# Taking GpSimd out of a four-layer graph network: its sums on VectorE, its powers as Ln and Exp on ScalarE with a Newton step

## The chip, the cores and the metric

The kernel runs on one core of a Trainium2 chip. The metric is the device time of one execution in microseconds, the median of several runs. The profile is one further execution, recorded instruction by instruction.

## The reference

32 independent graphs of 512 nodes with 256 features go through four layers. Each layer starts from `h = relu(layernorm(x))` and adds its result to `x`.

```python
# layers 0, 1, 2: attention over the neighbours (adj > 0), each with its own score
#   0: four heads, leaky_relu(e_src[i] + e_dst[j]), softmax over j, elu
#   1: one head, the same, but softmax over i, elu
#   2: scores h diag(a_k) h^T, leaky_relu, softmax over j
# layer 3: a transformer block over the symmetric adjacency
qkv = h @ Wqkv.T + bqkv                       # 8 heads of 32
attn = softmax(where(allowed, (q * scale) @ k.T, -inf))
x1 = layernorm(h + (attn @ v) @ Wo.T + bo) * g1 + b1
x2 = layernorm(x1 + relu(x1 @ W1.T + b1f) @ W2.T + b2f) * g2 + b2
```

A layernorm needs `(var + eps) ** -0.5` for each row. There are six per graph: one ahead of each of the four layers and the two inside layer 3.

## The kernel before, in words

One graph is 512 x 256 numbers, held as a tile of 128 partitions x 4 row blocks x 256. Everything of a graph stays on the chip. The body is written as a plan: `quick_path` (L307) calls `plan.dve`, `plan.act`, `plan.pool`, `plan.dma` and `plan.matmuls` (L213 to L240) for each step of each graph. Nothing is issued then. Each step takes the next number of the table `PLACES` (L265), and `carry_out` (L173) sorts the steps of all graphs by that number plus 100000 for each graph and issues them in that order. So the order on each engine is fixed by a table that was made beforehand from assumed durations (the arguments `fixed`, `each`, `takes`, `moves`); at run time each engine takes its own queue strictly in order and waits on semaphores. The numbers of one graph reach to five rounds of 100000, so that some five graphs are in flight at any time, in different layers. All instructions of the plan carry the line of the shared helper: L208 for VectorE, ScalarE and GpSimd, L240 for transposes and L242 for products on TensorE, L229 for the DMAs of the SP queue.

The places that the change touches:

- `norm_stats` (L418), called by `normed` (L433) for all six layernorms. VectorE takes statistics of the four row blocks (`st`, `mv`). GpSimd adds eps and raises to -0.5 (`rstd`, two instructions on 128 x 4). VectorE forms `shift` = -mean * rstd. ScalarE then applies `func(rstd * t + shift)` to each row block (`h`, `n` or `y`), and for five of the six norms TensorE transposes the result (`ps_t`).
- `layer2` (L599): GpSimd sets one column of `h` to 1.
- `layer3` (L646): GpSimd adds the bias rows to `h` and to `x`, multiplies `n` by the first gain and adds the first bias, multiplies `y` by the second gain and adds `x`. These are six instructions per graph on 128 x 1024 numbers.
- the heads of `layer3`, two groups (`g` = 0, 1) of four. For each of four blocks `j`: four score products into two PSUM tiles `ps_s`, two exponentials on ScalarE to `p`, one masking product on VectorE, then four products into `ps_ct` (the sums of values) and four with ones into `ps_to` (the softmax sums, each repeated on 32 partitions). ScalarE then copies `ps_to` to `to` and `ps_ct` to `cT`. The four distinct rows of `to` go through DRAM into a tile of 128 x 16 (`part`), VectorE inverts that, it goes through DRAM again and comes back repeated on 32 partitions by four DMAs (`inv<-in_d`), and VectorE multiplies `cT` by it. `ps_wo` is the product that follows.

PSUM holds two tiles for layers 0 to 2 (`ps_a`), two for layer 3 (`ps_b`), one `ps_ct` and one `ps_to`. Both `ps_b` tiles are taken by the scores of one block `j`.

A second path, `general_path`, runs only if a range check (`ok`) fails at the end. It does not run with these inputs.

Of the kernel before, what the change touches and what calls it, by code (L numbers as in the profile page):

```python
# [11 lines left out]
F32 = mybir.dt.float32  # L12
# [3 lines left out]
AF = mybir.ActivationFunctionType  # L16
OP = mybir.AluOpType
AX = mybir.AxisListType

P = 128  # L20
EPS = 1e-5
# [101 lines left out]
class Plan:  # L123
# [99 lines left out]
    def dma(self, out, in_, moves, takes=0.1, how="dma_start"):  # L223

        pairs = list(zip(out, in_)) if isinstance(out, list) else [(out, in_)]
        outs = [o for o, _ in pairs if isinstance(o, Part)]
        ins = [i for _, i in pairs if isinstance(i, Part)]
        real = lambda x: x.real() if isinstance(x, Part) else x
        call = lambda: [getattr(self.nc.sync, how)(real(o), real(i)) for o, i in pairs]  # L229
        return self.put("SP", takes * len(pairs), 0.1, outs, ins, call, moves=moves)  # L230
# [19 lines left out]
def cut(i, n):  # L250
    return slice(i * n, (i + 1) * n)
# [6 lines left out]
def width(args):  # L258
# [7 lines left out]
    5095, 0, 75421, 87257, 75421, 75422, 79730, 91873, 132389, 236254, 196081, 207636, 243857, 181976, 44107,  # L266
    34440, 42508, 30766, 53912, 52376, 46625, 51110, 60213, 60213, 60213, 70466, 70613, 70954, 70954, 70466,
    70613, 70954, 70955, 75749, 70466, 71304, 71304, 77395, 77395, 82751, 82751, 82751, 85231, 85616, 86620,
    87570, 88383, 87584, 87624, 87664, 87664, 90673, 88473, 88474, 90343, 90415, 90674, 90415, 94498, 90674,
    90674, 90675, 93427, 103844, 106136, 116456, 117561, 120303, 122479, 122479, 123102, 124701, 126554,  # L270
    118952, 128436, 123749, 129193, 132446, 132770, 134171, 134171, 134497, 134497, 125538, 135514, 135152,
    129427, 140054, 141849, 142365, 143295, 150203, 150647, 145729, 145510, 143627, 145727, 146676, 152577,
    152577, 154799, 155729, 155729, 160482, 161143, 161214, 199191, 252294, 161472, 170438, 163168, 161214,
    172243, 180822, 179815, 182438, 187335, 190423, 220320, 232349, 231107, 233547, 233849, 232349, 232349,
    233799, 233849, 233849, 234567, 235455, 235455, 235455, 237246, 238660, 238660, 238660, 237541, 238502,
    238502, 239837, 240015, 240584, 237049, 237247, 237247, 240584, 241849, 243910, 241849, 245067, 249595,
    249623, 249943, 256299, 263793, 272483, 276199, 251185, 257754, 261671, 261953, 275753, 249971, 249971,
    249971, 254481, 274656, 250485, 259697, 260833, 261106, 261106, 280063, 280063, 280502, 280588, 280588,
    280957, 280957, 281766, 282382, 283125, 280221, 279419, 284381, 281071, 281440, 284267, 283125, 283472,
    281561, 284267, 284087, 288386, 288386, 288386, 289738, 293577, 293577, 293145, 292388, 294294, 294650,  # L280
    294650, 295508, 295951, 296386, 296387, 296820, 297407, 295508, 298258, 298315, 298315, 299004, 299120,
    301865, 305936, 306664, 308000, 310488, 311544, 299530, 302461, 303130, 307485, 307981, 315988, 316802,
    318221, 312505, 310558, 310559, 316547, 317146, 318296, 321032, 321616, 318341, 308129, 308850, 313424,
    313654, 314031, 328211, 328128, 328971, 328971, 324764, 324951, 324951, 329855, 331034, 331034, 330095,
    332212, 332212, 350464, 363968, 329929, 325975, 334039, 341986, 331621, 325975, 336262, 347783, 347783,
    347783, 349528, 351433, 349793, 349596, 349528, 356201, 356201, 356202, 356822, 357899, 357954, 357954,
    360273, 360273, 362490, 363814, 363814, 363814, 363814, 363814, 363814, 364260, 364260, 375184, 377819,
    380031, 379751, 364470, 364941, 364941, 367324, 368254, 375151, 376257, 377227, 378857, 380372, 381525,
    381525, 381525, 384251, 383694, 381824, 383733, 382666, 387368, 389194, 390503, 386847, 389476, 387536,
    389476, 395301, 398014, 391945, 394211, 395296, 400302, 402208, 403099, 414392, 404840, 420693, 428278,  # L290
    428491, 430754, 431986, 433030, 399143, 399518, 399143, 406475, 409183, 415116, 404886, 411811, 410216,
    411811, 416520, 417484, 414099, 418232, 416703, 420289, 430404, 424852, 420322, 420706, 422850, 422850,
    432328, 425058, 425376, 432362, 429007, 430005, 430005, 431322, 432006, 433711, 364606, 433030, 434739,
    435922, 436329, 436329, 436344, 436344, 436344, 436345, 429961, 430544, 430005, 430005, 438443, 437988,
    440014, 440373, 440373, 440373, 441792, 441792, 441792, 442528, 442528, 442528, 442528, 442528, 442716,
    442529, 442529, 442529, 442529, 442529, 442529, 442806, 442823, 442823, 443009, 451286, 451286, 443789,
    443789, 443789, 446989, 448875, 447063, 450551, 451265, 451501, 453552, 456094, 453552, 447255, 448150,
    448695, 448695, 451068, 452896, 453703, 455669, 456461, 456752, 456909, 457770, 451242, 451242, 463337,
    463337, 463485, 463558, 463559, 463559, 463559, 463559, 463789, 463789, 463789, 463789, 463789, 463789,
    463789, 457995, 457995, 457995, 457995, 457995, 457996, 457996, 457996, 457996, 457996, 457996, 457996,  # L300
    458410, 458410, 458410, 458410, 458410, 463790, 463790, 458795, 458795, 463790, 463790, 458795, 458795,
    463790, 463790, 463790, 467483, 470996, 470996, 472513, 476280, 476333, 506480,
# [4 lines left out]
def quick_path(  # L307
# [5 lines left out]
    nc = tc.nc  # L313
    B, N, D = x.shape
    NT = N // P
# [26 lines left out]
    K |= {tag: Kind(act, tag, slots) for tag, slots in dict(st=8, mv=8, rstd=8, shift=8, spr=3).items()}  # L342
# [5 lines left out]
    def new(tag, name, shape, dtype=F32):  # L348
        return plan.tile(K[tag], name, shape, dtype)
# [6 lines left out]
    nhalf = const.tile([P, NT], F32, name="nhalf")  # L356
    nc.gpsimd.memset(nhalf, -0.5)
# [60 lines left out]
    def norm_stats(t):  # L418

        st = new("st", "st", [P, NT, 6])  # L420
        mv = new("mv", "mv", [P, NT, 2])
        for i in range(NT):
            plan.dve("bn_stats", st[:, i], t[:, i], fixed=0.4)
        for i in range(NT):
            plan.dve("bn_aggr", mv[:, i], st[:, i])
        rstd = new("rstd", "rstd", [P, NT])
        plan.pool("tensor_scalar_add", rstd, mv[:, :, 1], EPS, fixed=0.22)
        plan.pool("tensor_tensor", rstd, rstd, nhalf, OP.pow, fixed=1.03)
        shift = new("shift", "shift", [P, NT])
        plan.dve("scalar_tensor_tensor", shift, mv[:, :, 0], -1.0, rstd, OP.mult, OP.mult)  # L430
        return rstd, shift
# [51 lines left out]
    def masks(b, adj_t):  # L483
# [7 lines left out]
        for i in range(NT):  # L491
            plan.dma(mT[:, :, cut(i, P)], m[:, i], 0.5, 1.2, "dma_start_transpose")
# [106 lines left out]
    def layer2(b, x_t, mT):  # L599
        h = new("h1", f"h2_{b}", [P, NT, D + 1])  # L600
        plan.pool("memset", h[:, :, D], 1.0)
# [44 lines left out]
    def layer3(b, x_t, m3):  # L646
# [5 lines left out]
        plan.pool("tensor_add", h, h, bo_r.unsqueeze(1).to_broadcast([P, NT, D]))  # L652
# [23 lines left out]
        for g in range(KD):  # L676
            ps_ct = new("ps_ct", "ps_ct", [P, N])
            ps_to = new("ps_to", "ps_to", [P, N])
            for j in range(NT):
# [22 lines left out]
                plan.matmuls(0.98, *((ps_to[at], ones, p[:, r], j == 0, j == NT - 1) for r, at in enumerate(heads)))  # L702
            to = new("to", "to", [P, N])
            plan.act("copy", to, ps_to)
            plan.act("copy", cT[:, g], ps_ct)


# [4 lines left out]
            plan.dve("reciprocal", part, part, each=7.5e-3, fixed=0.13)  # L712
            parts.append(part)
            d2 = new("in_d", "in_d", [HG, N])
            plan.dma(d2.flat(lambda d: d.rearrange("r (q n) -> (r q) n", q=HD)), part, 0.05)
            inv = new("inv3", "inv3", [P, N])

            plan.dma(
                [inv[r * HD : (r + 1) * HD] for r in range(HG)],
                [d2[r].flat(lambda d, r=r: bass.AP(tensor=d.tensor, offset=d.offset, ap=[[0, HD], [1, N]])) for r in range(HG)],  # L720
                0.9,
            )
            plan.dve("tensor_mul", cT[:, g], cT[:, g], inv)
        plan.pool("tensor_add", x_t, x_t, b2_r.unsqueeze(1).to_broadcast([P, NT, D]))
# [16 lines left out]
        plan.pool("tensor_mul", n, n, g1_r.unsqueeze(1).to_broadcast([P, NT, D]))  # L741
        plan.pool("tensor_add", n, n, b1_r.unsqueeze(1).to_broadcast([P, NT, D]))
# [23 lines left out]
        plan.pool("tensor_mul", y, y, g2_r.unsqueeze(1).to_broadcast([P, NT, D]))  # L766
        plan.pool("tensor_add", y, y, x_t)
# [506 lines left out]
```

## Time and profile before

| what | value |
|---|---|
| median of 3 runs | 3963.26 us (3956.66 to 3964.89) |
| the profiled execution's own time | 3974.49 us |
| its span, first to last instruction | 3972.7 us |
| TensorE busy | 3757.4 us, 95% |
| VectorE busy | 2550.2 us, 64% |
| ScalarE busy | 1829.4 us, 46% |
| GpSimd busy | 772.2 us, 19% |
| mean share of the 16 DMA engines that the main queue takes | 12.8% |
| one graph to the next in the middle of the run (start of the mask step to the next) | 117.4 us |

A row of the groups gives line, engine, operation, names and shapes, count; then the busy time in us and the mean of one in ns; then the idle time of the engine just before these instructions and what ended it. "<-" in a wait reads "waited for". "issue" is idle time for which the profile shows no cause. In a timeline row the first number is the start in us, the second the time.

### The profile page before, as it was taken

The page shows a single profiled execution, that of the slowest core. Times are in us where ns is not written, and L with a number is a line of the kernel's source. Part 1 is how long each engine was busy: PE and PEld are TensorE (multiplying, and loading weights), DVE is VectorE, ACT ScalarE, POOL GpSimd, SP SyncE. Part 2 cuts the span into 40 slices and gives each one's busy share as a digit, 9 for nine tenths or more (in the row PEclk, how much of TensorE's full clock was granted, in tenths as well). Part 3 has the DMA queues.
Part 4 walks back from the last instruction along what each step waited for, and adds up shares of the span by engine and source line. Part 5 has one row for each costly group of instructions (what it writes and reads, how often), then busy time and mean ns, then how long its engine had stood idle before and what let it go on. Part 6 is the DMA issues. An engine that isn't in the chain of part 4 may idle for free. (4 is left out here: it accounts for less than half of the span.)

```text
span 3972.7 us, 51876 instructions
## 1 busy us (share of the span) xinstructions
PE 3757.4 (95%) x19974; PEld 2349.5 (59%) x19974; DVE 2550.2 (64%) x5083; ACT 1829.4 (46%) x3297; POOL 772.2 (19%) x618
## 2 busy tenths in 40 slices
PE   4899999999999999999999999999999999999986
PEld 3655666565666565566655566656566656566543
DVE  3576667766667676666776666676666776666532
ACT  1245444545444545544454544454544455454432
POOL 0012211212221121221121221121221121222121
PEclk7799999999999999999999999999999999999998
DMA  3111101111101111101111101111111111110000
GB/s 114 54 44 43 37 28 45 49 44 43 44 21 45 49 49 44 43 17 48 45 49 44 43 17 48 45 49 44 43 34 31 45 49 48 41 31 17 17 12 12
DMA packets 168911, 161.41 MB, mean 41 GB/s; under 512 B 98640, under 2 KB 134992, under 8 KB 164560
## 3 DMA queue, kind: packets, MB, share of 16 engines
q1 hardware_dynamic: 162304, 153.02, 12.8%
q10 hardware_dynamic: 6352, 4.99, 0.4%
q8 instruction: 160, 2.62, 0.3%
q14 instruction: 95, 0.78, 0.1%
HBM read 122.96 MB, written 18.22 MB: 36 GB/s over the span
## 5 line engine op out<-in xcount | busy, mean ns | idle before, releaser
L242 PEld LDWEIGHTS ps_o<-wh,p 128*128 128x128 f32 x5120 | 713.4, 199 | 157.8 <-issue 80.8
L242 PE MATMUL ps_o<-wh,p 128*128 128x65 f32 (+1 forms) x5120 | 761.1, 302 | 23.2 <-DVE p L208 21.2
L208 DVE TENSOR_TENSOR p<-p,m 128x2048 f32<-128x2048 f32 x256 | 585.6, 2288 | 74.1 <-ACT p L208 71.0
L208 ACT ACTIVATE p<-ps_s 128x1024 f32<-128x1024 f32 x512 | 506.3, 1024 | 213.6 <-PE ps_s L242 142.4
L242 PE MATMUL ps_f<-ff_t,f 128*128 128x256 f32 x2048 | 458.2, 380 | 36.2 <-DVE o L208 35.0
L208 POOL TENSOR_SCALAR rstd<-mv 128x4 f32<-128x4 f32 x192 | 47.8, 249 | 2276.8 <-DVE mv L208 2125.2
L242 PE MATMUL ps_f<-tT,ff_t 128*128 128x512 f32 x1024 | 481.2, 604 | 3.4 <-ACT tT L208 2.6
L242 PEld LDWEIGHTS ps_f<-ff_t,f 128*128 128x128 f32 x2048 | 381.9, 190 | 111.5 <-issue 61.2
L208 DVE SCALAR_TENSOR_TENSOR p<-rows,rt,mT 128x512 f32<-128x512 f32 x512 | 367.2, 744 | 42.3 <-PE ps_o L242 28.2
L208 ACT ACTIVATE h<-x,shift,rstd 128x256 f32<-128x256 f32 x512 | 274.9, 595 | 182.5 <-PE ps_o L242 144.0
L208 ACT ACTIVATE f<-ps_f,ff1b_c 128x512 f32<-128x512 f32 x256 | 164.4, 681 | 368.8 <-PE ps_f L242 368.7
L242 PE MATMUL ps_s<-qk 32*128 32x512 f32 x2048 | 295.1, 641 | 2.6 <-ACT qk L208 1.5
L242 PEld LDWEIGHTS ps_f<-tT,ff_t 128*128 128x128 f32 x1024 | 184.2, 192 | 170.5 <-issue 137.7
L242 PE MATMUL ps_to<-p,ones 128*32 128x512 f32 x2048 | 268.0, 606 | 6.0 <-DVE p L208 6.0
L242 PE MATMUL ps_ct<-p,v 128*32 128x512 f32 x2048 | 267.5, 606 | 5.2 <-DVE p L208 5.2
L208 POOL TENSOR_TENSOR rstd<-rstd,nhalf 128x4 f32<-128x4 f32 x192 | 258.0, 1348 | 13.4
L240 PE MATMUL ps_t<-ident,h 128*128 128x128 f32 x1024 | 203.8, 294 | 57.4 <-ACT h L208 38.7
L240 PEld LDWEIGHTS ps_t<-ident,h 128*128 128x128 f32 x1024 | 126.8, 146 | 208.7 <-ACT h L208 110.8
L208 DVE TENSOR_TENSOR u<-ps_f,n 128x512 f32<-128x512 f32 x64 | 43.7, 683 | 321.5 <-PE ps_t L240 284.3
L208 DVE SCALAR_TENSOR_TENSOR shift<-mv,rstd 128x4 f32<-128x4 f32 x192 | 161.0, 839 | 125.8 <-POOL rstd L208 125.8
L242 PE MATMUL ps_o<-h,p 128*128 128x257 f32 x1024 | 239.5, 386 | 0.9 <-DVE x L208 0.9
L242 PE MATMUL ps_qk<-h3T,wqkv_t 128*128 128x512 f32 x512 | 237.5, 597 | 1.1 <-ACT h3T L208 1.1
(114 smaller groups left out, 4885.8 us busy)
## 6 DMA issues: line engine op xcount, KB each, us to landing
adj<-in_adj_dram SPq DMA_DIRECT2D x32, 1024.0 KB
rows<-rows_d SPq DMA_DIRECT2D x32, 1024.0 KB
x<-in_x_dram SPq DMA_DIRECT2D x32, 512.0 KB
rows<-rows_d SPq DMA_DIRECT2D x32, 512.0 KB
inv<-in_d SPq DMA_DIRECT2D x256, 64.0 KB
out_dram<-y SPq DMA_DIRECT2D x32, 512.0 KB
ff_t<-in_L_gnn_W_dram ACTq DMA_DIRECT2D x2, 1024.0 KB
mT<-m SPq DMA_TRANSPOSE x128
```

The lines of the kernel that those rows point to most:

```text
L208: return [getattr(unit, method)(*map(real, args), **{k: real(v) for k, v in kw.items()})]
L240: made.append(self.nc.tensor.transpose(*map(real, c)))
L242: made.append(self.nc.tensor.matmul(*map(real, c[:3]), start=c[3], stop=c[4]))
```

## The change

All of it is inside `quick_path`. `PLACES` is a new table: another fixed order for all engines, made from the new assumed costs.

```diff
-    def dma(self, out, in_, moves, takes=0.1, how="dma_start"):
+    def dma(self, out, in_, moves, takes=0.45, how="dma_start"):
 PLACES = [
...
-    nhalf = const.tile([P, NT], F32, name="nhalf")
-    nc.gpsimd.memset(nhalf, -0.5)
+    eps = const.tile([P, 1], F32, name="eps")
+    nc.gpsimd.memset(eps, EPS)
...
         rstd = new("rstd", "rstd", [P, NT])
-        plan.pool("tensor_scalar_add", rstd, mv[:, :, 1], EPS, fixed=0.22)
-        plan.pool("tensor_tensor", rstd, rstd, nhalf, OP.pow, fixed=1.03)
+        plan.act("activation", rstd, mv[:, :, 1], AF.Ln, bias=eps, fixed=0.27)
+        plan.act("activation", rstd, rstd, AF.Exp, scale=-0.5)
+        r = new("newton", "newton", [P, NT])
+        plan.dve("scalar_tensor_tensor", r, mv[:, :, 1], EPS, rstd, OP.add, OP.mult)
+        plan.dve("scalar_tensor_tensor", r, r, -0.5, rstd, OP.mult, OP.mult)
+        plan.dve("scalar_tensor_tensor", rstd, r, 1.5, rstd, OP.add, OP.mult)
+
+        plan.dve("scalar_tensor_tensor", ok[:, :NT], mv[:, :, 1], 2.0**60, ok[:, :NT], OP.is_le, OP.mult)
         shift = new("shift", "shift", [P, NT])
...
-            plan.dma(mT[:, :, cut(i, P)], m[:, i], 0.5, 1.2, "dma_start_transpose")
+            plan.dma(mT[:, :, cut(i, P)], m[:, i], 0.5, 1.3, "dma_start_transpose")
...
-        plan.pool("memset", h[:, :, D], 1.0)
+        plan.dve("memset", h[:, :, D], 1.0)
...
-        plan.pool("tensor_add", h, h, bo_r.unsqueeze(1).to_broadcast([P, NT, D]))
+        plan.dve("tensor_add", h, h, bo_r.unsqueeze(1).to_broadcast([P, NT, D]))
...
+            last = g == KD - 1
+            inv = new("inv3", "inv3", [P, N])
+            if last:
+                for half in (slice(0, N // 2), slice(N // 2, N)):
+                    plan.dve("reciprocal", inv[:, half], ps_to[:, half], each=7.5e-3, fixed=0.13)
+                    plan.dve("tensor_mul", cT[:, g, half], ps_ct[:, half], inv[:, half])
             to = new("to", "to", [P, N])
             plan.act("copy", to, ps_to)
-            plan.act("copy", cT[:, g], ps_ct)
             d = new("to_d", "to_d", [HG, N])
             plan.dma(d, to.flat(lambda t: t[0:P:HD]), 0.3)
             part = new("part", "part", [P, N // HD])
             plan.dma(part, d.flat(lambda d: d.rearrange("r (q n) -> (r q) n", q=HD)), 0.2)
-            plan.dve("reciprocal", part, part, each=7.5e-3, fixed=0.13)
             parts.append(part)
-            d2 = new("in_d", "in_d", [HG, N])
...
-            plan.dma(
-                [inv[r * HD : (r + 1) * HD] for r in range(HG)],
...
-                0.9,
-            )
-            plan.dve("tensor_mul", cT[:, g], cT[:, g], inv)
-        plan.pool("tensor_add", x_t, x_t, b2_r.unsqueeze(1).to_broadcast([P, NT, D]))
+            if not last:
+                plan.act("copy", cT[:, g], ps_ct)
+                plan.dve("reciprocal", part, part, each=7.5e-3, fixed=0.13)
+                d2 = new("in_d", "in_d", [HG, N])
+                plan.dma(d2.flat(lambda d: d.rearrange("r (q n) -> (r q) n", q=HD)), part, 0.05)
+                plan.dma(
+                    inv, d2.flat(lambda d: bass.AP(tensor=d.tensor, offset=d.offset, ap=[[N, HG], [0, HD], [1, N]])), 2.9
+                )
+                plan.dve("tensor_mul", cT[:, g], cT[:, g], inv)
+        plan.dve("tensor_add", x_t, x_t, b2_r.unsqueeze(1).to_broadcast([P, NT, D]))
...
-        plan.pool("tensor_mul", n, n, g1_r.unsqueeze(1).to_broadcast([P, NT, D]))
-        plan.pool("tensor_add", n, n, b1_r.unsqueeze(1).to_broadcast([P, NT, D]))
+        plan.dve("tensor_mul", n, n, g1_r.unsqueeze(1).to_broadcast([P, NT, D]))
+        plan.dve("tensor_add", n, n, b1_r.unsqueeze(1).to_broadcast([P, NT, D]))
...
-        plan.pool("tensor_mul", y, y, g2_r.unsqueeze(1).to_broadcast([P, NT, D]))
-        plan.pool("tensor_add", y, y, x_t)
+        plan.dve("tensor_mul", y, y, g2_r.unsqueeze(1).to_broadcast([P, NT, D]))
+        plan.dve("tensor_add", y, y, x_t)
```

`takes`, `moves`, `fixed` and `each` are numbers of the plan alone; they reach no instruction. `newton` gets eight tiles of 128 x 4.

The built program shows one thing that the diff does not. ScalarE evaluates its functions from a loaded set of tables, and the build puts in the loads. The program before has one such load. The changed program has 384: one ahead of every Ln and one behind it, ahead of the Exp or of whatever else of the other set comes first. They name two different sets in turn. A stretch of ScalarE's queue in the middle of the run (number in the queue, operation, output <- input; this stretch has layer 3 of graph 5, layer 2 of graph 6, layer 0 of graph 8):

```
688 Activation p<-ps_s (twice, waits PE)
689 Activation wh_8<-ps_wh (waits PE)
690 LoadActFuncSet 5
691 Activation Ln rstd<-mv,eps (waits DVE)
692 LoadActFuncSet 0
693 Activation Exp rstd<-rstd
694 Activation rt<-ps_wh
695 Activation p<-ps_s (waits PE)
...
713 Activation p_5628<-ps_s, first half of the block
714 LoadActFuncSet 5
715 Activation Ln rstd<-mv,eps (waits DVE)
716 LoadActFuncSet 0
717 Activation p_5628<-ps_s, second half of the block
```

On the SP queue a graph has eight DMAs fewer: four of `inv<-in_d` and the `in_d<-part` of the last group, and three of the four `inv<-in_d` of the first.

## The prediction

> **What bounds the kernel now.** The page first: TensorE is busy 95% of the span and close to full in every slice but the first two and the last two.
>
> ```profile
> PE 3757.4 (95%) x19974; PEld 2349.5 (59%) x19974; DVE 2550.2 (64%) x5083; ACT 1829.4 (46%) x3297; POOL 772.2 (19%) x618
> ...
> PE   4899999999999999999999999999999999999986
> ```
>
> Then the waits of TensorE over two graphs in the middle (1526 to 1761 us). The two together are 4.7 us in two rounds of 117.4 us.
>
> ```profile
> PE ps_f L242 <- DVE o L208: 2.5, 2, 1.2
> PE ps_t L240 <- ACT h L208: 2.2, 6, 0.8
> ```
>
> So a round is 115 us of TensorE work and 2.4 us of waiting. No engine that is relieved can give back more than that: 32 x 2.4 = 77 us, plus some of the ramps. An engine that comes late can take any amount, because each queue is in fixed order. Third, one round in stretches, to see where ScalarE is dense (columns: stretch, length, then busy us and count for TensorE, its weight loads, VectorE, ScalarE, GpSimd; granted clock; DMA).
>
> ```profile
> 1536.00:1546.00 10.00, 10.00 (x63) 5.17 (x56) 9.59 (x18) 6.82 (x11) 2.61 (x4) 1.00 0.00 2
> 1546.00:1556.00 10.00, 10.00 (x62) 4.07 (x62) 6.61 (x13) 6.97 (x15) 2.02 (x2) 1.00 0.27 92
> 1556.00:1566.00 10.00, 10.00 (x61) 3.49 (x64) 8.62 (x10) 7.87 (x13) 0.00 (x0) 1.00 0.71 238
> ...
> sum 117.40, PE 114.92 PEld 71.68 DVE 79.71 ACT 57.18 POOL 24.18; mean PE 9.58 PEld 5.97 DVE 6.64 ACT 4.77 POOL 2.02
> ```
>
> ScalarE has 60 us free in a round, but in the 30 us of the softmax it is 72% busy, with VectorE at 83%. Fourth, the rows by shape that price the change.
>
> ```profile
> L208 DVE SCALAR_TENSOR_TENSOR shift<-mv,rstd 128x4 f32<-128x4 f32 x192 | 161.0, 839 | 125.8 <-POOL rstd L208 125.8
> L208 POOL TENSOR_TENSOR rstd<-rstd,nhalf 128x4 f32<-128x4 f32 x192 | 258.0, 1348 | 13.4
> L208 DVE SCALAR_TENSOR_TENSOR e<-e,x 128x1024 f32<-128x1024 f32 x32 | 38.6, 1206 | 1.1 <-ACT e L208 1.1
> L208 ACT ACTIVATE rt<-wh 128x4 f32<-128x4 f32 x96 | 16.1, 201 | 1.0
> L208 DVE RECIPROCAL part<-part 128x16 f32<-128x16 f32 x64 | 15.7, 245 | 7.0 <-DMA part<-to_d 6.8
> L208 DVE SCALAR_TENSOR_TENSOR ok<-inv,ok 128x4 f32<-128x4 f32 x64 | 9.0, 140 | 0.0
> L208 ACT ACT_TABLE_LOAD x1 | 1.3, 1283 | 26.2 <-DMA g_r<-in_L_gnn_ln_g_dram 26.2
> ```
>
> **What the Trainium skill says.** (1) "ScalarE: Activation LUTs", section "What ACT_TABLE_LOAD costs": a switch to another set takes 1283 ns for the load and some 1380 ns for a drain, 2.66 us in all. The load agrees with the row above. The one load here shows no drain: the next instruction starts 20 ns after its end.
>
> ```profile
> 26.15 1.28 ACT L208 ACT_TABLE_LOAD   x1 [26.15 <-DMA g_r<-in_L_gnn_ln_g_dram]
> 27.45 2.08 ACT L208 ACTIVATE h<-x,shift,rstd 128x256 f32<-128x256 f32 x4
> ```
>
> It stood behind an idle engine, though, so a drain of earlier work could not have shown. (2) Same page, "Table sets: the hidden batching unit": one set holds both exp and ln. The built program doesn't use that; its 384 loads alternate. (3) "TensorE: Matmul & The Clock Gate", Part 1: after about 3.4 us of idleness the array runs at half clock. The trace agrees. Near the end TensorE sits idle for 5.30 us, the stretch 3823 to 3826 shows a granted clock of 0.50, and 18 products that took 7.99 us a graph earlier take 9.63 us.
>
> ```profile
> 3823.22 2.17 PE L240 MATMUL ps_t<-ident,n 128*128 128x128 f32 x8 [5.30 <-ACT n L208]
> 3826.26 9.63 PE L242 MATMUL ps_f<-tT,ff_t 128*128 128x512 f32 x18 [0.87 <-ACT tT L208]
> ```
>
> **The change part by part**, for one graph (six norms).
>
> *Busy time.* ScalarE: 12 loads x 1.283 = 15.4 us, 6 Ln at 0.27 (a row with a pointer bias, `y<-ps_e,nshift`, less its elements) and 6 Exp at 0.2 = 2.8 us, less one `cT` copy of 0.58: 57.2 becomes 74.8 us of 117.4. VectorE: six sums of 1.2 = 7.2; two reciprocals of 256 numbers at (245-141)/15 = 6.9 ns each plus 0.14 = 3.8; two products from PSUM at 0.42 in place of one of 0.69 and a small reciprocal of 0.245, nothing; 18 Newton steps and 6 checks at 0.14 = 3.4; the memset 0.06. That is +14.4. Off go the waits for the port behind GpSimd: `shift` 839 instead of its median 161 ns, 6 x 0.68 = 4.1, and `mc<-rows,mT` 1183 instead of 690 (the `y<-y,y` of this size), 4 x 0.49 = 2.0. So 79.7 becomes 88. Neither engine passes TensorE's 115. GpSimd's work goes entirely; it was at 19% and costs nothing by going. The SP queue issues eight DMAs fewer a graph (of `in_d` and `inv`), and DMA is at 13%: nothing. Without the round trip through DRAM `ps_wo` of the last group can't wait for `inv<-in_d`. TensorE waited for `cT` 21 us in all, 12 of it in the last rounds: at most -10 us, and the reciprocals take VectorE time ahead of the same product; I take 0. The `takes` and `moves` only shape the new table.
>
> *Latency.* This is the price. Each norm puts load, Ln, load, Exp into a queue in fixed order. Behind them stand exponentials and ReLUs of other graphs, for which TensorE waits, and on VectorE the first Newton step holds everything behind it until the Exp is there. The table was made with Ln at 0.27 and Exp at 0.2 and no load, so its slack is not laid out for them. I went through one round of the new order, with TensorE's work between two points priced from the timeline of before (512 columns 0.87 us, 256 columns 0.43, four `ps_s` 1.07, four `ps_ct` or `ps_to` 1.0):
>
> - A, norm of layer 2: Ln waits for `mv` anyway, so the first load is covered by that; the second comes ahead of the exponentials of the third block. From those scores to `ps_to` TensorE has 5.2 us, the way over two exponentials (2.05), the mask product (2.29) and hand-overs takes 4.1. The load delays the first by 2.3 us: late by 1.3.
> - B, norm of layer 1, between the two exponentials of one block (queue numbers 713 to 717): 2 x 1.28 + 0.47 + 0.1 = 3.1 us against a slack of 5.0 - 4.1 = 0.9: late by 2.0.
> - C, first norm inside layer 3: `ps_wo`, sum, statistics, Ln, Exp, Newton, `n`, `ps_t`, in line with 6.1 us of other TensorE work as cover. The first load is hidden by the statistics, the second is not: 1.3, and 0.3 for hand-overs: 1.6.
> - D and E, norm of layer 3 and norm of layer 0, one shortly after the other between the ReLUs of the feed-forward: four loads, 5.1 us. TensorE wants the last `f` 4 to 5 us after its product is done: late by 1.0. `h` of both has over 10 us of cover.
> - F, last norm: nobody on TensorE waits for `y`, but the `qk` copies stand behind it. VectorE, held by E's Newton step for 5 us with about 1 us to spare, brings `u` late by 3; with F's own load `qk` comes 4 us late, less the 1 us by which TensorE is late already: 3.0.
>
> Sum: 1.3 + 2.0 + 1.6 + 1.0 + 3.0 = 8.9 us a graph, x 32 = 285 us. TensorE's old 2.4 us of waits may shrink as VectorE is freed of GpSimd; I take 0.5 x 32 = -16. No stall reaches 3.4 us, so I add nothing for the clock. 3974.5 + 269 = 4243 us for a profiled execution. The profiled one before was 11 us above the median of the runs (3963.3), so the forecast is 4232, rounded to 4230. The unknown is the switch: at 1.28 us at the low end, 2.66 at the high end of the skill. I take the low end, since the trace shows the next instruction 20 ns behind the load.
>
> **Rivals.**
> *The switch costs 2.66 us.* Twelve drains are 16.6 us of ScalarE a round; two fall where Ln waits. B becomes 4.8, C 3.0, A 2.7, D and E 6.0, F 4: 20.5 us x 32 = 656, and stalls of 4 us and more bring the half clock. 3963 + 640 = 4600, own range 4430 to 4850. For it: the skill's number. Against it: the 20 ns.
> *Less cover than counted.* VectorE is 83% busy in the softmax and is held by six Newton steps; lateness there passes on to the next block, since the two `ps_b` tiles are one block's. At 13 us a graph: 3963 + 416 = 4380. For it: the 83%. Against: every stall of TensorE also lets the others catch up.
> *Covered, and so not slower.* ScalarE is free for 60 us in a round, the loads need 15. If each lies where ScalarE waits for TensorE anyway, what counts is GpSimd's port waits, 6 us of VectorE a round, and the tail: up to -60 us, so 3900 to 3970, 3940 in the middle. It decides if the slack ahead of TensorE is over 2.6 us at all five places. Against it: B has 0.9.
> *The loads are merged or dropped*: then the same time as in the last case; the one load of before stands exactly where its program has it, so I give it little.
>
> **How the numbers follow.** Forecast 4230, own range 4090 to 4330 (4 to 11.5 us a graph): 0.62. Less cover, 4330 to 4430: 0.12. 2.66 us: 0.17. Between forecast and nothing, 3975 to 4090: 0.03. Covered or merged: 0.06. A range of 4090 to 4570 leaves out 0.09 below and about 0.1 above, half of the case of 2.66. Within 0.2% (8 us, what a measurement of this kernel can tell) lies little: 0.02 of the covered cases; faster 0.04; slower 0.94.
>
> **What would show it.** In the profile after: ACT_TABLE_LOAD x384 at 1283 ns, with ScalarE at some 2400 us busy; a pause of over 1 us between a load and its next instruction with nothing waited for would be the drain. A round of about 125.5 us, with TensorE waiting for `p` (A, B), `n` (C), `f` (D, E) and `qk` (F). `shift` at 160 ns, VectorE near 2800 us. It is wrong if TensorE's waits stay at 2.4 us a round, if they are on `cT` or `inv`, or if VectorE is busy where TensorE waits.

## The result and the profile after

The changed kernel takes 4111.0 us in the median (4109.2 to 4112.2), the kernel before 3963.0 beside it: a ratio of 1.038, 95% interval 1.036 to 1.039. It is 148 us slower, where 267 were forecast. The profiled execution took 4109.15 us, its span is 4107.7 us.

The page of the changed kernel, busy times and TensorE's slices:

```profile
PE 3831.2 (93%) x19974; PEld 2389.6 (58%) x19974; DVE 2728.4 (66%) x6139; ACT 2390.2 (58%) x4032; POOL 0.9 (0%) x10
...
PE   4799999999999999999999999999999999999886
```

GpSimd is empty, ScalarE went from 1829 to 2390 us, VectorE from 2550 to 2728. TensorE does the same 19974 products and is busy 74 us longer with them (3831.2 against 3757.4), so "busy" is not a measure of work alone. Most of the 74 us may be clock: the mean granted clock of the profiled execution fell from 0.976 to 0.961, which over the two spans is some 65 us more of lost clock (an estimate: 4107.7 x 0.039 less 3972.7 x 0.024).

TensorE's waits in three rounds of the changed kernel (1574.6 to 1944.7 us; total, times, longest):

```profile
PE ps_v L242 <- ACT qk L208: 7.9, 3, 2.6
PE ps_s L242 <- ACT p L208: 3.5, 3, 1.2
PE ps_t L240 <- ACT n L208: 1.9, 3, 0.6
```

A round waits 2.63 us for `qk` (F), 1.17 for `p` (B), 0.62 for `n` (C): 4.4 us. The old waits, for `o` and `h`, are gone. Some stretches of one of these rounds (stretch, length, busy us and count of TensorE, its weight loads, VectorE, ScalarE, GpSimd; clock; DMA):

```profile
1574.60:1580.00 5.40, 2.77 (x12) 2.09 (x11) 5.37 (x11) 5.29 (x12) 0.00 (x0) 0.92 0.30 60
1580.00:1585.00 5.00, 5.00 (x19) 4.12 (x18) 2.16 (x8) 3.57 (x8) 0.00 (x0) 0.75 0.21 40
...
1620.00:1630.00 10.00, 10.00 (x65) 6.26 (x65) 8.31 (x17) 4.80 (x6) 0.00 (x0) 0.83 0.08 27
...
1650.00:1660.00 10.00, 9.21 (x53) 7.35 (x52) 7.57 (x32) 7.89 (x14) 0.00 (x0) 0.88 0.01 2
...
sum 123.20, PE 118.56 PEld 73.90 DVE 84.25 ACT 73.76 POOL 0.00; mean PE 8.47 PEld 5.28 DVE 6.02 ACT 5.27 POOL 0.00
```

The clock column was 1.00 in the lines shown of before; in this round it falls behind each of the three stalls, though it does not do so in every round (see the last section). TensorE is busy 118.6 us a round, with the products of which the prediction said "115 us of TensorE work".

The rows by shape, against those that priced the change:

```profile
L208 ACT ACT_TABLE_LOAD x384 | 492.7, 1283 | 29.5 <-DMA g_r<-in_L_gnn_ln_g_dram 22.8
L208 DVE SCALAR_TENSOR_TENSOR newton<-mv,rstd 128x4 f32<-128x4 f32 x192 | 31.2, 162 | 425.6 <-ACT rstd L208 425.6
L208 DVE SCALAR_TENSOR_TENSOR shift<-mv,rstd 128x4 f32<-128x4 f32 x192 | 29.7, 154 | 2.3
L208 DVE RECIPROCAL inv<-ps_to 128x256 f32<-128x256 f32 x64 | 112.2, 1753 | 4.2 <-PE ps_to L242 2.0
```

384 loads at 1283 ns; `shift` at 154 ns; the reciprocal of 256 at 1.75 us (1.9 forecast); and VectorE stands 425.6 us, 13 us a graph, at the first Newton step. Last, ScalarE at B, the norm between two exponentials of one block:

```profile
1613.78 1.02 ACT L208 ACTIVATE p<-ps_s 128x1024 f32<-128x1024 f32 x1 [0.53 <-PE ps_s L242]
1614.82 1.28 ACT L208 ACT_TABLE_LOAD   x1
1616.11 0.30 ACT L208 ACTIVATE rstd<-mv,eps 128x4 f32<-128x4 f32 x1
1616.43 1.28 ACT L208 ACT_TABLE_LOAD   x1
1617.72 1.02 ACT L208 ACTIVATE p<-ps_s 128x1024 f32<-128x1024 f32 x1
```

Each load begins 20 ns after the work before it and is followed within 10 ns: the drain of 1380 ns that the Trainium skill gives in "ScalarE: Activation LUTs", section "What ACT_TABLE_LOAD costs", is not there, though these loads stand in a busy engine. The second half of `p` comes 2.9 us later than it could.

### The profile page after: what moved, and what is told of

Its sections match the earlier page's. It is cut to its first block, busy times and chain, and to the rows that moved or that the text cites. A ratio compares the mean times of both kernels' runs of the same rounds, so it can differ in the third digit from the quotient of the medians.

```text
span 4107.7 us, 52302 instructions
## 1 busy us (share of the span) xinstructions
PE 3831.2 (93%) x19974; PEld 2389.6 (58%) x19974; DVE 2728.4 (66%) x6139; ACT 2390.2 (58%) x4032; POOL 0.9 (0%) x10
## 4 chain that ended last, share of the span: by engine, by line
PE 62%; ACT 20%; DVE 12%; issue 3%; DMA 0%; ACTq 0%; DVEq 0%; SPq 0%
PE ps_o L242 20%; PE ps_f L242 12%; ACT L208 8%; PE ps_s L242 5%; ACT p L208 4%; PE ps_ct L242 4%; DVE p L208 4%; PE ps_v L242 4%; PE ps_to L242 4%; PE ps_e L242 4%; PE ps_wh L242 3%; PE ps_wo L242 3%; PE ps_t L240 2%; ACT rstd L208 2%; ACT y L208 2%
## 5 line engine op out<-in xcount | busy, mean ns | idle before, releaser
L242 PEld LDWEIGHTS ps_o<-wh,p 128*128 128x128 f32 x5120 | 696.6, 197 | 172.5 <-issue 93.6
L242 PE MATMUL ps_o<-wh,p 128*128 128x65 f32 (+1 forms) x5120 | 751.1, 301 | 22.5 <-DVE p L208 22.5
L208 ACT ACT_TABLE_LOAD x384 | 492.7, 1283 | 29.5 <-DMA g_r<-in_L_gnn_ln_g_dram 22.8
L242 PE MATMUL ps_f<-tT,ff_t 128*128 128x512 f32 x1024 | 466.3, 604 | 1.7 <-ACT tT L208 1.7
L242 PE MATMUL ps_s<-qk 32*128 32x512 f32 x2048 | 334.8, 645 | 36.2 <-ACT p L208 36.1
L208 DVE SCALAR_TENSOR_TENSOR newton<-mv,rstd 128x4 f32<-128x4 f32 x192 | 31.2, 162 | 425.6 <-ACT rstd L208 425.6
L242 PE MATMUL ps_ct<-p,v 128*32 128x512 f32 x2048 | 280.5, 621 | 5.0 <-DVE p L208 4.9
L242 PE MATMUL ps_v<-wqkv_t,h3T 128*128 128x256 f32 x512 | 162.5, 487 | 76.6 <-ACT qk L208 76.6
L242 PEld LDWEIGHTS ps_o<-h,p 128*128 128x128 f32 x1024 | 186.5, 189 | 77.6 <-DVE inv L208 26.0
L242 PEld LDWEIGHTS ps_s<-qk 32*128 32x128 f32 x2048 | 90.9, 183 | 224.7 <-ACT p L208 69.2
L208 DVE BATCH_NORM_STATS2 st<-x 128x6 f32<-128x256 f32 x512 | 205.1, 416 | 2.2
```

The costliest lines, as they stand in the source:

```text
L208: return [getattr(unit, method)(*map(real, args), **{k: real(v) for k, v in kw.items()})]
L242: made.append(self.nc.tensor.matmul(*map(real, c[:3]), start=c[3], stop=c[4]))
```

## The experiments

Two readings of the 148 us were open: the loads cost half of what was forecast and the rest of the change gives next to nothing, or the loads cost about what was forecast and the rest gives back far more than 16 us. Rounds below are means over 20 graphs, from one output sum (`t<-ps_wo,h`) to the next: 118.2 us before (the 117.4 of the prediction was a single one), 122.8 after.

### 1. The whole change with one table set

```diff
+    nc.scalar.preload_act_table_set("natural_log_exp_and_others")
     FULL, HALF = 0.862, 0.432
```

> The changed kernel with one line more: the set of tables that holds both Exp and Ln is loaded once at the start. The order of all other instructions is the same; 1 load in place of 384. If the loads are the cause (theory): TensorE's waits for qk, p and n and the half-clock windows behind them go, a round is 115 to 117.4 us, 3920 to 3975 us in all. If the work that VectorE got, or the new order itself, is the cause (rival): a round stays near 122.8 us, 4060 us or more.

Measured: 3794.0 us, ratio to before 0.956 (0.954 to 0.958), faster than either side had expected. The instructions and their order are those of the changed kernel, less 383 loads. The page of this kernel:

```profile
PE 3672.1 (97%) x19974; PEld 2332.3 (61%) x19974; DVE 2727.3 (72%) x6139; ACT 1899.2 (50%) x3649; POOL 0.9 (0%) x10
...
PE   4799999999999999999999999999999999999996
```

So the loads cost 4111 - 3794 = 317 us, and the rest of the change gains about 170: the first reading falls. A round takes 113.0 us, and over three rounds TensorE waits for nothing. Its busy time is 85 us less than in the kernel before, for the same products, and its idle time falls from 3972.7 - 3757.4 = 215 to 123 us. Half of the gain comes out of time that the page calls busy. Part of those 85 us is clock again (0.976 before, 0.982 here: some 27 us by the same estimate, most of it in the first and last graphs, since in the middle the kernel before has only 0.5 us a round at half clock). This is also the best version: 4.4% under the kernel before.

### 2. The loads alone, in the old order

```diff
         plan.pool("tensor_tensor", rstd, rstd, nhalf, OP.pow, fixed=1.03)
+        idle = new("newton", "newton", [P, NT])
...
+        plan.act("activation", idle, mv[:, :, 1], AF.Ln, bias=eps, fixed=0.27)
...
+        plan.act("activation", idle, idle, AF.Exp, scale=-0.5)
```

> The kernel before, with its order, its GpSimd powers and its GpSimd sums, plus one Ln and one Exp per norm on ScalarE whose results nobody uses: 384 loads in a queue that was laid out without them. Theory: 3 to 8 us a graph, 4060 to 4220 us. Rival (VectorE's work or the new order): within 15 us of 3963.

Measured: 4355.4, ratio 1.098 (1.095 to 1.100): 387 us for the same 384 loads, with the Ln and Exp that they belong to, and above all that was expected. Its waits over three rounds:

```profile
PE ps_sp L243 <- ACT rt L211: 15.6, 3, 5.2
PE ps_t L243 <- ACT n L211: 5.2, 3, 1.7
PE ps_v L245 <- ACT qk L211: 4.9, 3, 1.6
PE ps_f L245 <- ACT f L211: 3.1, 3, 1.1
```

The price of one load is the same, 1283 ns, but others wait for it: here the longest wait is one that neither kernel has in the middle of its run. A round grows from 118.2 to 129.9 us; TensorE's idle time in it goes from 2.9 to 10.0 us, and 12.0 us of it are at half clock. What a load costs depends on its place in the queue.

### 3 to 5. Which norms the loads hurt

One norm or two take Identity in place of Ln, so their loads go; the queue is otherwise the same. These three kernels leave out the power in those norms and do not compute the reference's result; they serve to find the place of the cost.

```diff
-        y = normed(u, new("n", f"y_{b}", [P, NT, D]), AF.Identity)
+        y = normed(u, new("n", f"y_{b}", [P, NT, D]), AF.Identity, AF.Identity)
```

> The changed kernel with Identity in place of Ln in the last norm of a graph (F) alone, so that this norm causes no load; its rstd is then not the power -0.5. 320 loads. If TensorE's wait for qk (2.63 us a round) and the half-clock window behind it (3.41 us at half rate, 1.7 us) both come of it: -4.3 us a graph, near 3980 us. If the wait alone: near 4030. If each pair of loads costs its share of the 148 us: near 4086.

Measured: 4014.6, ratio 1.012 (1.009 to 1.014): 96 us less for 64 loads. The wait for `qk` falls from 2.63 to 0.93 us; those for `p` and `n` stay. The time lies between the reading of the wait alone (4030) and that of the wait with the clock (3980).

```diff
-        h = normed(x_t, new("h0", f"h0_{b}", [P, NT, D]), AF.Relu)
+        h = normed(x_t, new("h0", f"h0_{b}", [P, NT, D]), AF.Relu, AF.Identity)
...
-        h = normed(x_t, new("h3", f"h3_{b}", [P, NT, D]), AF.Relu)
+        h = normed(x_t, new("h3", f"h3_{b}", [P, NT, D]), AF.Relu, AF.Identity)
```

> The changed kernel with Identity in place of Ln in the norms of layer 3 and of layer 0 (D and E), so that these cause no load; their rstd is then not the power -0.5. 257 loads. TensorE waits at neither place. Theory: they hold VectorE at the first Newton step of E for 4.9 us, which makes u late for the last norm; without them 2.2 of the 2.63 us of the wait for qk go, and the half-clock window with it: -3.5 to -4 us a graph, 3985 to 4010 us. Rival (what TensorE doesn't wait for costs nothing): 4100 to 4115 us.

Measured: 3982.9, ratio 1.004 (1.003 to 1.005): 128 us less. TensorE never waited for D or E, yet they cost 128 us (the theory's 3985 to 4010, and 2 us more), since without them the wait for `qk` is gone altogether. The changed kernel's VectorE shows the way:

```profile
1682.06 0.16 DVE L208 SCALAR_TENSOR_TENSOR newton<-mv,rstd 128x4 f32<-128x4 f32 x1 [4.90 <-ACT rstd L208]
...
1692.63 0.68 DVE L208 TENSOR_TENSOR u<-ps_f,n 128x512 f32<-128x512 f32 x1
1694.87 0.68 DVE L208 TENSOR_TENSOR u<-ps_f,n 128x512 f32<-128x512 f32 x1
```

VectorE is held for 4.90 us at E's Newton step, what follows is late, and the last norm starts late. F and D with E share one wait, which either alone does most to end: their two gains can't be added. No run leaves out the loads of A or C alone.

```diff
-        h = normed(x_t, new("h1", f"h1_{b}", [P, NT, D + 1]), AF.Relu)
+        h = normed(x_t, new("h1", f"h1_{b}", [P, NT, D + 1]), AF.Relu, AF.Identity)
```

> The changed kernel with Identity in place of Ln in the first norm of layer 1 alone (B of the prediction), so 320 table loads in place of 384; the output is not the reference's, as that norm is wrong. The changed kernel took 4111. If a load costs what TensorE is seen to wait for behind it: 1.17 us a round for p, and the half clock behind that stall some 1.7 us, so 2.9 us x 32 = 93 us, 4018. If loads cost by their own time alone, the two that go give 2.6 us x 32 = 82 us, 4029. If the prediction's 2.0 us for B holds, 64 us, 4047. If the next stall takes up what this one gives: 4080 or more.

Measured: 4003.7, ratio 1.008 (1.007 to 1.010): 107 us less, nearest to the reading with the clock (93). The round falls by 3.4 us: 1.17 of wait, 1.1 of clock (5.6 us at half clock become 3.4), and about 1.1 in time counted as busy.

### 6. What the new order gains, and what an empty GpSimd

The order with GpSimd as full as before; then only the powers on it; then only the sums.

```diff
-        plan.act("activation", rstd, mv[:, :, 1], AF.Ln, bias=eps, fixed=0.27)
-        plan.act("activation", rstd, rstd, AF.Exp, scale=-0.5)
...
+        plan.pool("tensor_scalar_add", rstd, mv[:, :, 1], EPS, fixed=0.22)
+        plan.pool("tensor_tensor", rstd, rstd, nhalf, OP.pow, fixed=1.03)
+        plan.at += 3
...
-        plan.dve("tensor_add", h, h, bo_r.unsqueeze(1).to_broadcast([P, NT, D]))
+        plan.pool("tensor_add", h, h, bo_r.unsqueeze(1).to_broadcast([P, NT, D]))
```

(and so for the other sums and the memset)

> The changed kernel's order and its inversion of the last heads from PSUM, with GpSimd as loaded as before: its powers (an addition and a power per norm) and its six sums and the memset go back to GpSimd, at the places that the new table gives to the steps they replace; no Ln, no table load, no Newton step. The kernel with one table set took 3794, the kernel before 3963 to 3968. Theory P ([...]an empty GpSimd is the gain): this stays near the kernel before, 3920 to 3980, with shift at 600 ns or more. Theory O (the gain of some 170 us is the new order, with the round trip through DRAM gone): 3790 to 3850. A value of 3860 to 3910 says both have a share.

> The changed kernel's order, only the powers go back to GpSimd (an addition and a power of 128 x 4 per norm, 1.35 us for the power in the kernel before); the sums stay on VectorE; no Ln, no table load, no Newton step. Beside the kernel with one table set (3794). Theory P: GpSimd works 192 times for 1.6 us, some 10 us a graph in place of 24[...]: 3820 to 3870. Theory O: 3790 to 3810, since the power's 1.6 us stands against 0.5 us of Ln and Exp and 0.5 us of Newton steps, and VectorE has 29 us of slack in a round.

> The kernel with one table set, in which only the six sums of 128 x 1024 and the memset of each graph go back from VectorE to GpSimd; powers stay on ScalarE with the Newton step, one table load in the whole kernel. Theory P: [...]VectorE's two-operand steps beside it are stretched: 3830 to 3900. Theory O: 3790 to 3820; VectorE is relieved of 7 us of work a graph and the sums take 2 us each instead of 1.2, none of which TensorE waits for.

Measured, beside 3966.6 for the kernel before: 3864.9, ratio 0.974 (0.972 to 0.977); 3808.3, 0.960 (0.957 to 0.963); 3800.4, 0.958 (0.956 to 0.961). So the order with its inversion from PSUM gains 102 us with a full GpSimd, and emptying GpSimd 71 more. Of those, freeing it of the sums alone brings 57, of the powers alone 65: either nearly suffices. With both on GpSimd, TensorE waits 1.08 us a round for `qk`, and steps of VectorE are stretched beside a busy GpSimd, `shift` taking 533 ns:

```profile
L208 DVE SCALAR_TENSOR_TENSOR shift<-mv,rstd 128x4 f32<-128x4 f32 x192 | 102.3, 533 | 141.8 <-POOL rstd L208 141.8
```

With the powers alone on GpSimd it takes 154 ns:

```profile
L208 DVE SCALAR_TENSOR_TENSOR shift<-mv,rstd 128x4 f32<-128x4 f32 x192 | 29.7, 154 | 146.0 <-POOL rstd L208 146.0
```

But stretched steps are not what decides. With the sums alone on GpSimd VectorE is busy 2825 us, though six sums a graph have left it (2727 with them in the kernel of experiment 1), because other steps are stretched; this one takes 1218 ns in the kernel of experiment 1:

```profile
L208 DVE SCALAR_TENSOR_TENSOR e<-e,x 128x1024 f32<-128x1024 f32 x32 | 99.6, 3111 | 1.0 <-ACT e L208 1.0
```

TensorE still waits for nothing in the middle of the run, and the time is only 6 us above 3794.

### 7. GpSimd empty in the old order

Ln and Exp stand at the places of the addition and the power, the Newton steps and the check at that of the power, every sum where it was but on VectorE, and the table set is loaded once.

```diff
-        plan.pool("tensor_scalar_add", rstd, mv[:, :, 1], EPS, fixed=0.22)
-        plan.pool("tensor_tensor", rstd, rstd, nhalf, OP.pow, fixed=1.03)
+        plan.act("activation", rstd, mv[:, :, 1], AF.Ln, bias=eps, fixed=0.27)
+        plan.act("activation", rstd, rstd, AF.Exp, scale=-0.5)
...
-        plan.pool("tensor_add", h, h, bo_r.unsqueeze(1).to_broadcast([P, NT, D]))
+        plan.dve("tensor_add", h, h, bo_r.unsqueeze(1).to_broadcast([P, NT, D]))
...
```

> The kernel before in its own order and with its inversion through DRAM, GpSimd emptied in its graphs: Ln and Exp at the places of the addition and the power, the three Newton steps and the check behind them on VectorE, the sums and the memset on VectorE at the places they had on GpSimd; the table set that holds both functions is loaded once. Theory P: most of the gain comes without the new order: 3800 to 3870. Theory O: 3930 to 3990 (the order was made for GpSimd's times). If the old order puts a sum of 1.2 us ahead of something that TensorE waits for on VectorE, it may even be slower than the kernel before, up to 4020.

Measured: 3965.3, ratio 0.9995 (0.998 to 1.001): nothing. The rows show that the hindrance is gone all the same (`shift` 839 to 161 ns, `mc` 1183 to 678):

```profile
L211 DVE SCALAR_TENSOR_TENSOR shift<-mv,rstd 128x4 f32<-128x4 f32 x192 | 30.8, 161 | 0.0
L211 DVE TENSOR_TENSOR mc<-rows,mT 128x512 f32<-128x512 f32 x128 | 84.0, 678 | 3.7 <-DMA rows<-rows_d 3.7
```

TensorE's waits changed places: those for `h` (1.1 us a round) are gone and that for `o` fell from 1.2 to 0.9, but 0.7 for `qk` and 0.5 for `spr`, a copy on VectorE, are new. So in this order the relief and the work that came to VectorE and ScalarE cancel; what each is worth there, no run shows.

### 8. Order and inversion, one without the other

The inversion from PSUM put into the old order by hand, with GpSimd as before and then with it empty:

```diff
-            plan.act("copy", cT[:, g], ps_ct)
...
+            if last:
...
+                for i, half in enumerate((slice(0, N // 2), slice(N // 2, N))):
...
+                    plan.dve("reciprocal", inv[:, half], ps_to[:, half], each=7.5e-3, fixed=0.13)
...
+                    plan.dve("tensor_mul", cT[:, g, half], ps_ct[:, half], inv[:, half])
...
+            else:
+                plan.act("copy", cT[:, g], ps_ct)
```

> The kernel before in its own order, GpSimd as it was; only the last heads' sums are inverted from PSUM in two halves on VectorE, with the two products from PSUM, all four at the place of ScalarE's copy of cT, which goes, as do the second trip through DRAM, the small reciprocal and the product of that group. The new order with GpSimd loaded as before took 3865, the kernel before 3967 beside it. Theory I (the inversion is what the new order gains by): 3860 to 3900. Theory O (it is the order of the whole queues): 3940 to 3990, since TensorE's waits of the old order are for o and h, and for cT only in the last rounds (some 10 us there).

> The kernel before in its own order with every part of the change but the new order: GpSimd empty in the graphs, Ln, Exp and Newton steps on one table set, sums on VectorE, and the last heads' sums inverted from PSUM at the place of the old copy. The old order with GpSimd empty took 3965; the same parts in the new order 3794. Theory I: 3850 to 3900. Theory O: 3930 to 3990, that is, all of the 170 us need the new order. If the two reciprocals of 1.75 us, put into VectorE's old queue by hand, hold what TensorE waits for, up to 4030.

Measured: 4156.9, ratio 1.047 (1.045 to 1.048), and 4155.5, 1.047 (1.045 to 1.049). Both theories expected less; the hand-placed halves make `cT` late. Emptying GpSimd beside them again brings nothing (1.4 us). Of the first of the two, TensorE's waits over three rounds, and two-microsecond stretches from that wait on:

```profile
PE ps_wo L245 <- DVE cT L211: 10.0, 3, 3.3
PE ps_f L245 <- DVE o L211: 3.7, 3, 1.3
PE ps_t L243 <- ACT h L211: 3.3, 9, 0.8
```

```profile
1658.00:1660.00 2.00, 0.25 (x1) 0.25 (x2) 1.70 (x2) 0.00 (x0) 0.00 (x0) 0.91 0.00 0
1660.00:1662.00 2.00, 2.00 (x9) 1.72 (x9) 0.56 (x1) 0.00 (x0) 0.00 (x0) 0.50 0.00 0
1662.00:1664.00 2.00, 2.00 (x11) 2.00 (x11) 0.79 (x3) 0.00 (x0) 0.00 (x0) 0.50 0.00 0
1664.00:1666.00 2.00, 2.00 (x9) 1.71 (x9) 1.22 (x4) 0.00 (x0) 0.00 (x0) 0.50 0.00 0
```

A stall of 3.34 us, then over 6 us at half clock: the round grows by 6.4 us, more than the stall.

The other way round, the new order with the old way through DRAM:

```diff
-            if last:
-                for half in (slice(0, N // 2), slice(N // 2, N)):
-                    plan.dve("reciprocal", inv[:, half], ps_to[:, half], each=7.5e-3, fixed=0.13)
-                    plan.dve("tensor_mul", cT[:, g, half], ps_ct[:, half], inv[:, half])
...
+            if last:
...
+                plan.dve("reciprocal", part, part, each=7.5e-3, fixed=0.13)
...
+                plan.act("copy", cT[:, g], ps_ct)
...
+                plan.dve("tensor_mul", cT[:, g], cT[:, g], inv)
```

> The changed kernel's order with GpSimd empty and one table set (3794), but the last heads' sums take the way of the kernel before again: to and cT are copied from PSUM by ScalarE, the sums go through DRAM, are inverted in 128 x 16, come back through DRAM, and one product makes cT; each step stands at the place of the step that it replaces, the last product at that of the last product. In the kernel with one table set TensorE ends the last sums at 1626.6 us and takes the last output product from 1634.1, 7.5 us later; in the kernel before the way through DRAM took from 1578.9 to 1589.9, 11 us. Theory O (the whole order is the gain, and the inversion adds nothing to it): 3790 to 3815. Theory I (the new order stands only with the short way): TensorE waits 3 to 5 us a round for cT, and what a stall of that length takes from the clock comes on top: 3794 + 32 x 3.5 to 32 x 7, so 3905 to 4020.

Measured: 4007.4, ratio 1.010 (1.008 to 1.012), 213 us above the same kernel with the inversion from PSUM; theory I holds, at the upper end. TensorE's waits over three rounds, then VectorE at that product:

```profile
PE ps_wo L245 <- DVE cT L211: 10.6, 3, 3.6
```

```profile
1705.96 0.24 DVE L211 RECIPROCAL part<-part 128x16 f32<-128x16 f32 x1
1713.51 0.69 DVE L211 TENSOR_TENSOR cT<-cT,inv 128x512 f32<-128x512 f32 x1 [7.30 <-DMA inv<-in_d]
```

So, at the places I gave the steps by hand, the new order stands only with the short way, and the short way only with the new order. The 102 us belong to the two together, and with them goes a small part that no run takes out: `inv` of the first group comes by one DMA in place of four. How the gain would divide with places made for each is left open.

## Why the forecast was right in sign and too high in size

The sum, by its own terms (us for the whole kernel):

| term | forecast | measured | by |
|---|---|---|---|
| the loads | +285 | +317 | changed kernel less one set, experiment 1 |
| relief by the rest | -16 | about -170 | one set less before, experiment 1 |
| all | +267 | +148 | the result |

The time lies at the low end of the forecast's range, 4090 to 4330, but not for the reason that end stands for, which is loads at some 4 us a graph: they cost 9.8. That the whole came out there is luck, since the relief that was missed stood against them.

**The step that failed** is "No engine that is relieved can give back more than that: 32 x 2.4 = 77 us, plus some of the ramps", and the 16 us taken from it. The recorded waits were read as the whole of what TensorE lost, and its busy 115 us as work. The work is at most 113.0 us a round, as the kernel with one set shows, so the round of before held 5.2 us too much, not 2.4. Over the same 20 graphs 2.9 us of them are recorded idle time; the other 2.3 lie in time counted as busy. Start to start, without the recorded idle time, the transposes of `h` fell from 4.6 to 3.7 us a round; smaller amounts, 0.3 us or less each, lie in `ps_f<-tT,ff_t`, `ps_e`, `ps_y`, `ps_v` and others. Transposes of one `h` of layer 0, before and then with one set:

```profile
1526.82 0.82 PE L240 MATMUL ps_t<-ident,h 128*128 128x128 f32 x3 [0.78 <-ACT h L208]
1527.80 0.33 PE L240 MATMUL ps_t<-ident,h 128*128 128x128 f32 x1 [0.16 <-ACT h L208]
1528.29 0.55 PE L240 MATMUL ps_t<-ident,h 128*128 128x128 f32 x3 [0.17 <-ACT h L208]
```

```profile
1571.52 0.60 PE L240 MATMUL ps_t<-ident,h 128*128 128x128 f32 x4
...
1573.67 0.60 PE L240 MATMUL ps_t<-ident,h 128*128 128x128 f32 x4
```

Four in a row take 0.60 us; of those that follow ScalarE's pieces of `h`, one alone takes 0.33. The groups of the whole run, before and then with one set, agree:

```profile
L240 PE MATMUL ps_t<-ident,h 128*128 128x128 f32 x1024 | 203.8, 294 | 57.4 <-ACT h L208 38.7 <-DVE st L208 11.9 <-DVE h1T L208 4.5
```

```profile
L240 PE MATMUL ps_t<-ident,h 128*128 128x128 f32 x1024 | 155.1, 280 | 27.2 <-ACT h L208 26.7 <-DVE mv L208 0.5
```

The same 1024 transposes cover 204 us in one kernel and 155 in the other, with nearly the same mean: while they arrive one by one behind `h`, much of the time between them counts as busy. (A group's time overlaps with that of the products that follow its own, so the 49 us are not all TensorE's gain.)

A second part of that step failed too: the relief was looked for in the engines ("as VectorE is freed of GpSimd"). Experiment 7 puts that, with the work that came in its place, at nothing in the old order. The line "The `takes` and `moves` only shape the new table" passed over the table itself: a new order of all queues, with the inversion it was made for, gains 102 us, and in that order an empty GpSimd is worth 71 more.

**The loads**: size nearly right (9.8 us a round against 8.9), split wrong, and so in part by luck: the waits that were counted came to half, and the clock and TensorE's busy time, for which nothing was added, made up for it. (B's own sum, 3.1 less 0.9, gives 2.2 and not 2.0; that is 6 us in all.)

- TensorE's waits: 4.4 us, not 8.9. F 2.63 (3.0 forecast), B 1.17 (2.0), C 0.62 (1.6), A nothing (1.3). The new order had more cover than the places I counted from the timeline of before.
- D and E: "late by 1.0" for `f`, measured nothing; but their hold on VectorE, which the step under F names, is real and costs as much as any (experiment 4).
- The clock: "No stall reaches 3.4 us, so I add nothing" failed. The changed kernel's TensorE spends 5.6 us a round at half clock, so up to 2.8 us are lost; the kernel before spends 0.5, the kernel with one set none. The Trainium skill, "TensorE: Matmul & The Clock Gate", Part 1, sets the fall after an idle window of about 3.4 us; here stalls of 2.63 us and less were followed by it. The trace of before had a sign of that: from 3870.6 us on the clock is 0.50 for 6.4 us, behind stalls of 1.47 and 1.11 us. The same 16 products after the stall for `qk`, in the changed kernel and in that with one set (3.62 us):

```profile
1577.99 5.41 PE L242 MATMUL ps_v<-wqkv_t,h3T 128*128 128x256 f32 x16 [2.63 <-ACT qk L208]
```

```profile
1574.11 3.62 PE L242 MATMUL ps_v<-wqkv_t,h3T 128*128 128x256 f32 x16
```

- The remaining 2.6 us or more of the 9.8 lie in TensorE's busy time, again as products that wait one by one; that they are only this is argued, not shown.

**The rivals.** The switch at 2.66 us fell with the pauses of 10 to 20 ns. "Less cover" pointed the wrong way. "Covered" was right that the relief is worth more than 16 us (up to 60 by its count, about 170 measured), and wrong about the loads. The busy times (ScalarE "some 2400", VectorE "near 2800"), the counts and `shift` came as said; the round came at 122.8, not 125.5.

## What to carry to other kernels

An engine that is 95% busy in a profile may still have several per cent to give: compare the busy time of the same instructions in two orders before you call it work, and don't take the recorded waits as the ceiling of a gain. Where queues run in a fixed order, relief on one engine can be worth nothing until the order is made anew, as here in experiment 7, and a path made shorter can cost more than it saves in an order that was not made for it. And look at which table sets a program loads: one preload of a set that holds both functions was worth 317 us here, twice what the whole change seemed to lose.

## What the runs showed of the hardware

- Half clock came in the middle of the run in stretches of 3.41 us or two or three of them, behind stalls far shorter than that. Over 22 rounds of the changed kernel it followed the stall of 2.63 us 21 times, that of 1.17 us 15 times and that of 0.62 us once. Length alone does not decide: the stall of 1.25 us for `o` in the kernel before, that of 1.08 us in the first of experiment 6 and that of 1.63 us in experiment 2 were followed by none in as many rounds. The stall of 3.34 us (experiment 8) was always followed by 6.83 or 10.24 us at half clock. What decides is open.
- A table load in a busy ScalarE costs its 1283 ns, and the next instruction follows within 10 to 20 ns; with Ln and Exp alternating and no preload, the program loaded 384 times, with the joint set preloaded once.
- VectorE's single steps are stretched by much beside a busy GpSimd (839 against 161 ns for 128 x 4, 3111 against 1218 for 128 x 1024). Emptying GpSimd was worth nothing or 71 us, by the order around it.
